# Four resident groups ordered by one account of all engines, and a Strassen-form LSTM step, in a four-layer fp32 graph network kernel

## The chip, the cores and the metric

The kernel runs on one core of one Trainium2 chip. The metric is the device time of one execution in microseconds (us), given as the median of several runs. All arithmetic is fp32. The engines are TensorE (PE in the profile, with its weight loads as PEld), VectorE (DVE), ScalarE (ACT), GpSimd (POOL) and SyncE (SP), which issues the transfers.

## What is computed

The input is 128 graphs of 64 nodes with 256 features, 8192 rows in all, and one 64 x 64 adjacency matrix. Four layers follow each other, each of the form "x = layernorm(x + layer(x))". Cut to what matters, with `mix` for the product over the 64 nodes:

```python
# layer 0: three convolutions with adj*adj, 256 -> 512 -> 1024 -> 256
h = relu(mix(adj*adj, x @ W1)); h = relu(mix(adj*adj, h @ W2)); y = mix(adj*adj, h @ W3)
# layer 1: U holds the eigenvectors of a normalised Laplacian of adj
y = mix(U, relu(mix(U.T, x) @ W1 + b1) @ W2 + b2)
# layer 2: two convolutions, then for p = 1..4 an LSTM over windows of p node rows
h = relu(mix(adj, x @ Wg0 + bg0)); h = relu(mix(adj, h @ Wg1 + bg1))
for p in 1, 2, 3, 4:                       # the last state replaces the last row of each window
    for t in range(p):
        i, f, g, o = split(x_t @ Wih[p].T + hs @ Whh[p].T + bias)
        c = sigmoid(f) * c + sigmoid(i) * tanh(g); hs = sigmoid(o) * tanh(c)
# layer 3: attention over the 64 nodes, masked by adj
h = x @ W + b_lin; y = softmax(where(adj, h @ h.T * adj, -1e16)) @ h + b
```

## The kernel before

The 8192 rows are 64 tiles of 128 rows (two graphs each), and four tiles make a group, so there are 16 groups. All 64 tiles stay in SBUF, in `X`.

**Stage one** (to about 860 us in the profile) does layer 0 for all groups in turn, two groups overlapping, while DVE works through the eigenvectors (`eigen`). Layer 0's big product already has Strassen's form: seven products of quarter matrices in place of eight.

**Stage two** does layers 1, 2 and 3 for each group. The functions are generators, `layer1` (L962), `layer2` (L1057), `lstm` (L992) and `layer3` (L1102), and `group` (L1188) runs them for one group. A loop at the end of the kernel keeps `WAYS = 3` generators going. It counts PE's time in `now[0]`: `mm` (L715 to L718) adds two passes of each matmul, and every `yield` says from when the generator can go on. The stated delays are constants (`MOVE, MIXED, LIN, CONV, NORM, SOFT` and `CELL`), so PE's order is written out by an account of PE alone, in which the other engines are fixed delays. DVE, ACT and POOL are not in it (`manual_schedule(engines={PE})`): their order comes from the tile framework. The last two groups are in `ENDING`; their layer 3 is split into two halves so that the end has more pieces to interleave.

Line L716 is the helper through which nearly all matmuls go. An fp32 matmul leaves two records in the profile, a transpose (L926) one. In the LSTM, L1030 is the tanh of a gate out of PSUM on ACT, L1034 to L1041 are the cell's products on DVE, and L1051 writes the last state into `hT`. One step with t > 0 makes, for each of two halves h of the hidden units and each of four gates, two matmuls with `wih` and two with `whh` into one PSUM tile. For p = 2, 32 windows of 8 rows give n = 256 moving columns, so the second step of that pass is 32 matmuls of 256 columns for each group. A norm is bn_stats and bn_aggr on DVE (L551, L552), two steps on POOL (L553, L554) and the scaling on DVE (L564).

PSUM has eight tiles of one bank each (512 fp32 values for each partition), `ps`. In this kernel every `ps` tile is first written completely by PE and then read.

Of the kernel before, what the change touches and what calls it, by code (L numbers as in the profile page):

```python
# [1 line left out]

# [13 lines left out]
N = 64  # L16
# [24 lines left out]
class Timed:  # L41
# [6 lines left out]
    def __getattr__(self, name):  # L48
        def give(out, *args, **kw):
            self.free[0] = max(self.free[0], self.until[0]) + self.least + 0.0009 * max(0, np.prod(out.shape[1:]) - 64)  # L50
            return getattr(self.engine, name)(out, *args, **kw)  # L51

        return give

# [479 lines left out]
P = 128  # L534
D = 256
EPS = 1e-5
WAYS = 3
ENDING = (14, 15)
LEAD = 10
# [57 lines left out]
def kernel(  # L597
# [51 lines left out]
    X = keep.tile([P, NT, D], F32, name="X")  # L649
# [4 lines left out]
    nc.scalar.dma_start(X[:, 2:4, :], x_t[:, 2:4, :])  # L654
    for t in range(2):
        nc.sync.dma_start(X[:, t, :], x_t[:, t, :])
# [6 lines left out]
    for t in range(4, NT, 2):  # L663
        nc.sync.dma_start(X[:, t:t + 2, :], x_t[:, t:t + 2, :])
# [79 lines left out]
    def layer0(g):  # L744
        xs = X[:, 4 * g:4 * g + 4, :]
# [108 lines left out]
        for t in (2, 0):  # L854
            p = tl(psa, [P, 2, D], "ps", bufs=6)
            mm(p, sqT2, s3[:, t:t + 2, :])
            yield now[0]
            x2 = xs[:, t:t + 2, :]
            VL.tensor_add(x2, p, x2)
            norms.extend(scalar_norm(tc, small, x2, half, spare))  # L860

# [45 lines left out]
    pg = ctx.enter_context(tc.tile_pool(name="pg", bufs=WAYS, reuse_waits="tile"))  # L907
    pw = ctx.enter_context(tc.tile_pool(name="pw", bufs=5, reuse_waits="tile"))
    pv = ctx.enter_context(tc.tile_pool(name="pv", bufs=4, reuse_waits="tile"))
    psb = ctx.enter_context(tc.tile_pool(name="psb", bufs=8, space=bass.MemoryType.PSUM, reuse_waits="tile"))  # L910
# [10 lines left out]
    now[0] = due[0] = 0.0  # L921
    MOVE, MIXED, LIN, CONV, NORM, SOFT = 1.2, 1.2, 1.5, 1.8, 5.2, 5.2
    CELL = {256: 3.8, 168: 2.2, 128: 1.9}

    def turn(out, in_):
        PE.transpose(out, in_, ident)  # L926
        now[0] += 0.11

    def work():
        return tl(pw, [P, 1024], "w")  # L930

    def work2():
        return tl(pv, [P, 512], "v")

    spare[0] = lambda: work2()[:, :D]

    def ps4(shape=(P, 512)):
        return tl(psb, list(shape), "ps")
# [4 lines left out]
    def mixed(src, rhs, ready):  # L943

        dst = as3(work(), 2)
        ps = [ps4() for _ in range(2)]
        for t in range(4):
            if t % 2 == 0:
                yield ready[t // 2]
            for c in range(2):  # L950
                mm(ps[c][:, t * P:(t + 1) * P], src[:, t, c * P:(c + 1) * P], rhs)
        with tc.high_priority(offset=1500):
            V.tensor_copy(dst[:, 0, :], ps[0])
        S.copy(dst[:, 1, :], ps[1])
        yield now[0] + MIXED
        return dst

    def norm(xs, t, ready, more=0.0, scalar=False):
        rows_norm(tc, small, xs[:, t:t + 2, :], half, scalar)
        ready.append(now[0] + NORM + more + (0.8 if ready else 0.0))  # L960

    def layer1(xs, ready):  # L962
        a = yield from mixed(xs, u2, ready)
        for t in range(0, 4, 2):
            V.tensor_add(xs[:, t:t + 2, :], xs[:, t:t + 2, :], ub2.unsqueeze(1).to_broadcast([P, 2, D]))
        h = as3(work2(), 4)
        for t in range(0, 4, 2):
# [5 lines left out]
            yield now[0]  # L973
        yield now[0] + LIN
        z = work2()
        p = ps4((P, 4, P))
        for t in range(4):
            mm(p[:, t, :], h[:, t, :], ut2)
        S.copy(as3(z, 4), p)
        yield now[0] + MOVE  # L980
        ready = []
        for t in range(0, 4, 2):
            p = ps4((P, 2, D))
            for j in range(2):
                mm(p[:, j, :], z[:, (t + j) * P:(t + j + 1) * P], bw2)
            V.tensor_add(xs[:, t:t + 2, :], p, xs[:, t:t + 2, :])  # L986
            norm(xs, t, ready, 2.0)
            yield now[0]
        return ready

    def lstm(hT, p, first, nw):
# [6 lines left out]
        for t in range(p):  # L998
# [4 lines left out]
            G = tl(pg, [P, 2048], "gates")[:, :2 * len(names) * n].rearrange("p (q h n) -> p q h n", h=2, n=n)  # L1003
            gate = {q: G[:, i] for i, q in enumerate(names)}
            units = [(h, q) for h in range(2) for q in names]

            ahead = {}
            early = units[:2] if t else []
            for h, q in early:
                m = slice(("ifgo".index(q) * 2 + h) * P, ("ifgo".index(q) * 2 + h + 1) * P)  # L1010
                ahead[h, q] = pp = ps4()[:, :n]
                for k in range(2):
                    mm(pp, wi[:, k, m], xt[k], k == 0, False)
            if t:
                yield ready
            if p > 1 and not t:
                c = tl(pg, [P, 512], "c")[:, :2 * n].rearrange("p (h n) -> p h n", h=2)
            new = None if last else tl(pg, [P, 512], "hs")[:, :2 * n].rearrange("p (h n) -> p h n", h=2)
            for h, q in units:
                j = 2 * "ifgo".index(q) + h  # L1020
                m = slice(j * P, (j + 1) * P)
                pp = ahead.get((h, q))
                if pp is None:
                    pp = ps4()[:, :n]
                    for k in range(2):
                        mm(pp, wi[:, k, m], xt[k], k == 0, k == 1 and not t)
                if t:
                    for k in range(2):
                        mm(pp, wh[:, k, m], hs[:, k, :], False, k == 1)
                S.activation(gate[q][:, h, :], pp, AF.Tanh, bias=bias[:, j:j + 1], scale=0.5 if q == "g" else 0.25)  # L1030
                if q == "g":
                    to = gate["g"][:, h, :] if t or p == 1 else c[:, h, :]
                    if t:
                        V.scalar_tensor_tensor(c[:, h, :], gate["f"][:, h, :], 1.0, c[:, h, :], op0=ALU.add,  # L1034
                                               op1=ALU.mult)
                    V.scalar_tensor_tensor(to, gate["i"][:, h, :], 1.0, gate["g"][:, h, :], op0=ALU.add, op1=ALU.mult)  # L1036
                    if t:
                        V.scalar_tensor_tensor(c[:, h, :], c[:, h, :], 0.5, to, op0=ALU.mult, op1=ALU.add)  # L1038
                    S.activation(gate["i"][:, h, :], c[:, h, :] if p > 1 else to, AF.Tanh, scale=0.5)  # L1039
                if q == "o" and not last:  # L1040
                    V.scalar_tensor_tensor(new[:, h, :], gate["o"][:, h, :], 1.0, gate["i"][:, h, :], op0=ALU.add,  # L1041
                                           op1=ALU.mult)
                if q == "o":
                    if h == 0:
                        yield now[0]
                elif h == 1 or len(units) == 8:
                    yield now[0]
            if last:

                for h in range(2):  # L1050
                    V.scalar_tensor_tensor(hT[:, h, slice(first + p - 1, first + nw * p, p), :],  # L1051
                                           gate["o"][:, h, :].rearrange("p (w b) -> p w b", b=8), 1.0,
                                           gate["i"][:, h, :].rearrange("p (w b) -> p w b", b=8), op0=ALU.add,
                                           op1=ALU.mult)
            ready = now[0] + CELL[n]
            hs = new
        return ready  # L1057

    def layer2(xs, g, ready):
        a = yield from mixed(xs, adT2, ready)  # L1060
        g1 = as3(work(), 4)
        ready = []
        for t in range(0, 4, 2):
            p = ps4((P, 2, D))
            for j in range(2):
                run(p[:, j, :], [(a[:, k, (t + j) * P:(t + j + 1) * P], cw0[:, k, :]) for k in range(2)])
            V.tensor_add(g1[:, t:t + 2, :], p, wide["c_b0"].unsqueeze(1).to_broadcast([P, 2, D]))
            relu(g1[:, t:t + 2, :], g1[:, t:t + 2, :])
            ready.append(now[0] + CONV)
            yield now[0]  # L1070
        a = yield from mixed(g1, adT2, ready)
        hT = tl(pw, [P, 1024], "w").rearrange("p (k n b) -> p k n b", k=2, b=8)
        for c in range(2):
            p = ps4((P, 4, P))
            run(p, [(cw1[:, k, c * P:(c + 1) * P], a[:, k, :]) for k in range(2)])
            h = work2()
            V.scalar_tensor_tensor(as3(h, 4), rs_row.unsqueeze(1).to_broadcast([P, 4, P]), cb1[:, c:c + 1], p,
                                   op0=ALU.mult, op1=ALU.add)
            S.activation(hT[:, c, :, :].rearrange("p n b -> p b n"), as3(h, 8), AF.Relu, scale=2.0)
            yield now[0]  # L1080
        ready = now[0] + CONV
        for p, first, nw in ((1, 0, 32), (1, 32, 32), (2, 0, 32), (3, 0, 21), (4, 0, 16)):
            if first == 0:
                yield ready
            ready = yield from lstm(hT, p, first, nw)
        hb = as3(work(), 2)
# [175 lines left out]
```

## Time and profile before

| what | value |
|---|---|
| median of 3 runs | 2536.85 us (2536.6 to 2537.04) |
| the profiled execution | 2540.87 us |
| its span, first to last instruction | 2539.1 us |
| granted TensorE clock, mean | 0.993 |
| DVE, ACT in the stretch 910 to 1195 us | 119.05 and 136.85 us busy of 285 |
| POOL's norm steps L553 and L554 | 284 and 705 ns each |
| group outputs to DRAM | 28 transfers of 256 KB, 8 of 128 KB, 2.1 and 1.7 us to landing |

The profile is one execution; its span stands for the chip's work and the 1.8 us around it are start and end. Busy PE time covers each record from start to a modelled end, and records overlap: a record of 128 columns is 275 ns long, but the next one starts about 112 ns after it. What a matmul costs is therefore read from the distance between starts, and short gaps on PE are hidden in the overlap.

### The profile page before, as it was taken

How to read it: one execution, taken by the hardware profiler on the slowest of the kernel's cores; microseconds unless marked ns; L12 is line 12 of the kernel's file. 1: busy time of each engine (PE TensorE's matmuls, PEld its weight loads, DVE VectorE, ACT ScalarE, POOL GpSimd, SP SyncE). 2: the span in 40 equal slices, each digit the busy share in tenths (PEclk: the TensorE clock that was granted, in tenths of full speed). 3: DMA queues.
4: the chain of work that ended last, by engine and by line, in shares of the span. 5: the costliest groups of instructions: out<-in, count | busy, mean ns of one | idle time of the engine just before them, and what ended most of it. 6: DMA issues, size and time to landing. Idle time of an engine off the chain costs nothing.

```text
span 2539.1 us, 39015 instructions
## 1 busy us (share of the span) xinstructions
PE 2494.8 (98%) x15020; PEld 2196.2 (86%) x15020; DVE 1407.8 (55%) x4996; ACT 1090.6 (43%) x2706; POOL 134.2 (5%) x316
## 2 busy tenths in 40 slices
PE   9999999999999999999999999999999999999997
PEld 7788887888878889998989889898998998978996
DVE  6888777778885433454453543544445345353235
ACT  2344333433333344445344444444444534535454
POOL 0000000000000100000000000000000000010001
PEclk9999999999999999999999999999999999999998
DMA  6000000000000300000000000000000000000000
GB/s 219 1 1 1 1 1 1 1 1 1 1 1 1 117 1 1 10 9 1 9 9 1 9 1 10 9 1 9 1 9 9 1 9 9 1 9 1 1 1 26
DMA packets 24634, 32.09 MB, mean 13 GB/s; under 512 B 2176, under 2 KB 21376, under 8 KB 24448
## 3 DMA queue, kind: packets, MB, share of 16 engines
q1 hardware_dynamic: 24096, 29.32, 3.4%
q8 instruction: 118, 1.93, 0.3%
q14 instruction: 68, 0.56, 0.1%
q10 hardware_dynamic: 352, 0.28, 0.0%
HBM read 21.20 MB, written 8.39 MB: 12 GB/s over the span
## 4 chain that ended last, share of the span: by engine, by line
PE 91%; DVE 5%; POOL 2%; issue 1%; DMA 0%; ACT 0%; SPq 0%; ACTq 0%; POOLq 0%; DVEq 0%
PE ps L716 88%; PE ps L926 2%; POOL ln_rs L554 1%; DVE X L564 1%; DVE ln_st L551 1%; DVE D L51 1%; PE ps L1146 1%; PE pc L93 1%; DMA X<-in_x_dram 0%; POOL ln_rs L553 0%; DVE tw L51 0%; DVE ln_mv L552 0%; DVE X L1176 0%; DVE X L986 0%; DVE X L1096 0%
## 5 line engine op out<-in xcount | busy, mean ns | idle before, releaser
L716 PE MATMUL ps<-w,wih 128*128 128x256 f32 (+2 forms) x4992 | 894.0, 319 | 1.8 <-DVE w L1051 1.8
L716 PEld LDWEIGHTS ps<-w,wih 128*128 128x128 f32 x4992 | 760.9, 191 | 47.8 <-issue 5.7
L1030 ACT ACTIVATE gates<-ps,cbi 128x128 f32<-128x128 f32 (+2 forms) x1248 | 499.3, 410 | 523.3 <-PE ps L716 516.2
L716 PE MATMUL ps<-hs,whh 128*128 128x128 f32 (+2 forms) x3072 | 540.5, 303 | 6.2 <-DVE hs L1041 6.2
L716 PEld LDWEIGHTS ps<-hs,whh 128*128 128x128 f32 x3072 | 453.9, 191 | 32.9 <-issue 11.2
L1036 DVE SCALAR_TENSOR_TENSOR gates<-gates 128x256 f32<-128x256 f32 (+2 forms) x256 | 89.3, 349 | 297.4 <-ACT gates L1030 297.4
L716 PE MATMUL ps<-aw,h 128*128 128x256 f32 x1024 | 227.2, 379 | 0.0
L716 PEld LDWEIGHTS ps<-aw,h 128*128 128x128 f32 x1024 | 192.9, 190 | 25.9 <-ACT h L725 0.5
L725 ACT ACTIVATE h<-h 128x512 f32<-128x512 f32 x128 | 80.5, 629 | 170.0 <-DVE h L51 169.8
L1039 ACT ACTIVATE gates<-c 128x128 f32<-128x128 f32 (+2 forms) x288 | 98.1, 341 | 114.1 <-DVE c L1038 87.9
L1034 DVE SCALAR_TENSOR_TENSOR c<-gates,c 128x128 f32<-128x128 f32 (+2 forms) x192 | 62.6, 326 | 139.4 <-ACT gates L1030 138.2
L1051 DVE SCALAR_TENSOR_TENSOR w<-gates 128x256 f32<-128x256 f32 (+2 forms) x160 | 59.6, 376 | 108.5 <-PE ps L716 73.5
L716 PE MATMUL ps<-ss,tw 128*128 128x256 f32 x512 | 117.9, 380 | 0.0
L716 PE MATMUL ps<-ss,aw 128*128 128x256 f32 x512 | 117.3, 379 | 0.0
L716 PE MATMUL ps<-m,aw 128*128 128x256 f32 x512 | 117.1, 380 | 0.0
L716 PE MATMUL ps<-aw,m 128*128 128x512 f32 x256 | 114.8, 594 | 0.0
L1041 DVE SCALAR_TENSOR_TENSOR hs<-gates 128x128 f32<-128x128 f32 (+2 forms) x192 | 62.6, 326 | 93.6 <-ACT gates L1039 52.4
L553 POOL TENSOR_SCALAR ln_rs<-ln_mv 128x2 f32<-128x2 f32 x96 | 26.2, 273 | 1558.4 <-DVE ln_mv L552 1557.9
L716 PEld LDWEIGHTS ps<-ss,aw 128*128 128x128 f32 x512 | 96.6, 190 | 12.8
L716 PEld LDWEIGHTS ps<-ss,tw 128*128 128x128 f32 x512 | 96.3, 190 | 12.9 <-issue 0.2
L564 DVE TENSOR_SCALAR X<-X,ln_mv,ln_rs 128x256 f32<-128x256 f32 x176 | 64.7, 410 | 75.9 <-POOL ln_rs L554 75.9
L716 PEld LDWEIGHTS ps<-m,aw 128*128 128x128 f32 x512 | 95.6, 190 | 12.6 <-issue 0.5
(294 smaller groups left out, 3107.4 us busy)
## 6 DMA issues: line engine op xcount, KB each, us to landing
X<-in_x_dram SPq DMA_DIRECT2D x30, 256.0 KB, 6.3
out_dram<-X SPq DMA_DIRECT2D x28, 256.0 KB, 2.1
wih<-in_c_ih_dram SPq DMA_DIRECT2D x4, 1024.0 KB, 7.2
aw<-in_a_w_dram SPq DMA_DIRECT2D x3, 1024.0 KB, 10.3
whh<-in_c_hh_dram SPq DMA_DIRECT2D x3, 1024.0 KB, 9.4
out_dram<-X SPq DMA_DIRECT2D x8, 128.0 KB, 1.7
aw<-in_a_w_dram SPq DMA_DIRECT2D x1, 512.0 KB, 5.8
cw<-in_c_w_dram SPq DMA_DIRECT2D x2, 256.0 KB, 5.1
```

The source lines that it names most:

```text
L51: return getattr(self.engine, name)(out, *args, **kw)
L553: nc.gpsimd.tensor_scalar(rs, mv[:, :, 1], EPS, None, op0=ALU.add)
L564: nc.vector.tensor_scalar(x[:, t, :], x[:, t, :], mv[:, t, 0:1], rs[:, t:t + 1], op0=ALU.subtract, op1=ALU.mult)
L716: PE.matmul(out, lhsT, rhs, start=start, stop=stop)
L725: S.activation(dst, src, AF.Relu)
L926: PE.transpose(out, in_, ident)
L1030: S.activation(gate[q][:, h, :], pp, AF.Tanh, bias=bias[:, j:j + 1], scale=0.5 if q == "g" else 0.25)
L1034: V.scalar_tensor_tensor(c[:, h, :], gate["f"][:, h, :], 1.0, c[:, h, :], op0=ALU.add, op1=ALU.mult)
L1036: V.scalar_tensor_tensor(to, gate["i"][:, h, :], 1.0, gate["g"][:, h, :], op0=ALU.add, op1=ALU.mult)
L1039: S.activation(gate["i"][:, h, :], c[:, h, :] if p > 1 else to, AF.Tanh, scale=0.5)
L1041: V.scalar_tensor_tensor(new[:, h, :], gate["o"][:, h, :], 1.0, gate["i"][:, h, :], op0=ALU.add, op1=ALU.mult)
L1051: V.scalar_tensor_tensor(hT[:, h, slice(first + p - 1, first + nw * p, p), :], gate["o"][:, h, :].rearrange("p (w b) -> p w b", b=8), 1.0, ...
```

## The change

It has four parts.

1. **One account.** The generators become plain functions which only note operations. `Noted` stands in for an engine and passes each call to `Plan.note` with a duration; `Plan.run` then takes, again and again, the operation that can start earliest on any engine by the account's own clocks, emits it, and advances that engine. PE, DVE, ACT and POOL all follow the account's order (`manual_schedule` now names all four). Which operation must wait for which is found from the elements of a tile that each one touches (`mask`), and tiles get their buffers (`slots`) in the account too. A run of one product's matmuls (`run`) is one entry.
2. **Four groups on the way**, `WAYS = 4`, with gate tiles of half the size. `X` holds 32 tiles. Stage one works on groups 8 to 15 first, writes each finished one to a DRAM buffer (`rest`) and loads groups 0 to 7 in its place (`change`); stage two takes groups 0 to 7 first and loads a waiting group back when one is finished (`Q.dma_start(xs, rest[g])`).
3. **The second step of p = 2 in Strassen's form** (`second`): windows are cut into two halves of 128 columns and the gates into two pairs; `add_weights` makes four sums of weight blocks once (eight DVE additions of 512 columns), and for each group eight DVE subtractions of 128 columns make the moving operands. For each half h seven products follow, each of two gates, 128 columns and two addends (`wih`, `whh`). `two` puts two products into one PSUM tile, products (1, 2), (6, 7), (5, 3) and then 4 alone; one ACT copy and seven DVE additions of 256 columns put them together, and the tanh reads the sums from SBUF.
4. **Small things.** Layer 1's second mixing is noted by pairs of tiles, the copy before layer 2's transposes is cut in two by batches, each output tile is a transfer of its own, and layer 3's transposes for `hn` come after the scores. What is left of stage one's norms (`left_over`) is handed to the account as a group 0.

```diff
+class Plan:
+    LAG = {"PE": 0.205, "DVE": 0.16, "ACT": 0.15, "POOL": 0.0, "SP": 2.0}
+    MOST = {"w": 3, "v": 2, "ps": 4, "gates": 2}
+    OWN = {"PE": 0.0, "DVE": 0.125, "ACT": 0.105, "POOL": 0.0, "SP": 0.0}
...
+    def note(self, engine, calls, cost, ready=0.0):
...
+                t, write = x.tile, i == 0
+                mask = np.zeros(int(np.prod(t.shape[1:])), bool)
+                mask[x.at.reshape(-1)] = True
+                for other, w, rows, m in t.past:
+                    if (w or write) and other is not op and other.start is None and rows[0] < x.rows[1] and x.rows[0] < rows[1] and (m & mask).any():
+                        op.before.add(other)
...
+    def run(self, groups, ways):
...
+                if first:
+                    t0 = min(t for t, _ in first)
+                    t, op = min((x for x in first if x[0] <= t0 + 0.02), key=lambda x: (rank(x[1]), x[1].rank))
+                    if best is None or t < best[0]:
+                        best = t, op
...
+            self.emit(op)
...
-WAYS = 3
+WAYS = 4
...
-    X = keep.tile([P, NT, D], F32, name="X")
+    X = keep.tile([P, NT - 4 * LATE, D], F32, name="X")
...
+        def change():
+            nc.sync.dma_start(rest[g], xs)
+            for t in (0, 2):
+                nc.sync.dma_start(xs[:, t:t + 2, :], given(order[g + LATE])[:, t:t + 2, :])
...
+    def second(hT, xt, hs, c, bias):
...
+        moving = ((x1[0], h1[0]), (x2[0], h2[0]), (x2[1], h2[1]), T4, T1, T2, T3)
+        weight = (0, 1, 6, 2, 3, 4, 5)
+        for h in range(2):
...
+            def two(*which):
+                p = ps4((P, 2, 2, P))
+                for at, i in enumerate(which):
+                    for q in range(2):
+                        run(p[:, at, q, :], [(ways[s][weight[i]][:, q, h, :], moving[i][s]) for s in range(2)])
+                return p[:, 0], p[:, 1]
+            p1, p2 = two(0, 1)
+            S.copy(u1, p1)
+            V.tensor_add(a, u1, p2)
+            p6, p7 = two(5, 6)
+            V.tensor_add(c12, u1, p6)
+            V.tensor_add(b, c12, p7)
+            p5, p3 = two(4, 2)
+            V.tensor_add(d, b, p5)
+            V.tensor_add(c12, c12, p5)
+            V.tensor_add(c12, c12, p3)
+            p4, _ = two(3)
+            V.tensor_add(b, b, p4)
...
-    with tc.manual_schedule(engines={mybir.EngineType.PE}):
...
+    with tc.manual_schedule(engines={mybir.EngineType.PE, mybir.EngineType.DVE, mybir.EngineType.Activation,
+                                     mybir.EngineType.Pool}):
+        plan.run([left_over] + [lambda g=g: group(g) for g in range(NT // 4)], WAYS)
```

## The prediction

> **What bounds the kernel now.** I read the page's first part and the chain of waits first.
>
> ```profile
> span 2539.1 us, 39015 instructions
> ...
> PE 2494.8 (98%) x15020; PEld 2196.2 (86%) x15020; DVE 1407.8 (55%) x4996; ACT 1090.6 (43%) x2706; POOL 134.2 (5%) x316
> ...
> PE 91%; DVE 5%; POOL 2%; issue 1%; DMA 0%; ACT 0%; SPq 0%; ACTq 0%; POOLq 0%; DVEq 0%
> ```
>
> PE is the bound: 98% busy, 91% of the chain that ended last. Work taken from PE shortens the time, and every new PE wait lengthens it. Next, by windows, where PE is not busy in stage two (columns: window, length, then busy time of PE, PEld, DVE, ACT, POOL, granted clock, DMA share, GB/s):
>
> ```profile
> 860.00:910.00 50.00, 45.87 (x273) 40.41 (x272) 29.28 (x73) 22.53 (x51) 7.70 (x18) 0.93 0.26 105
> ...
> 1200.00:1436.00 236.00, 235.72 (x1561) 213.26 (x1561) 110.14 (x310) 106.80 (x263) 13.63 (x28) 1.00 0.02 8
> 1436.00:1442.00 6.00, 3.92 (x30) 3.43 (x28) 4.53 (x17) 1.27 (x4) 2.43 (x4) 1.00 0.02 5
> ...
> 2255.00:2271.00 16.00, 10.25 (x57) 9.69 (x56) 8.34 (x24) 3.46 (x8) 3.12 (x6) 0.68 0.06 20
> 2271.00:2500.00 229.00, 228.16 (x1567) 213.28 (x1565) 86.58 (x257) 112.20 (x287) 8.30 (x20) 1.00 0.01 2
> 2500.00:2532.00 32.00, 23.09 (x147) 17.51 (x145) 18.66 (x66) 14.86 (x38) 5.38 (x16) 0.79 0.08 25
> ```
>
> PE stands still only at four kinds of place: the stage change, five group boundaries (1436 to 1442 is one; the others are like it, 2.1 to 2.4 us idle each), the boundary before the last groups, and the end. DVE is under half busy between them.
>
> What a matmul costs is read from starts in PE's timeline (start, busy, records):
>
> ```profile
> 1511.95 2.75 PE L716 MATMUL ps<-w,wih 128*128 128x256 f32 x12
> 1514.54 0.27 PE L926 MATMUL ps<-ident,w 128*128 128x128 f32 x1
> ...
> 2471.76 1.06 PE L716 MATMUL ps<-hs,whh 128*128 128x128 f32 x8
> 2472.66 0.59 PE L716 MATMUL ps<-w,dw 128*128 128x512 f32 x1
> ```
>
> Twelve records of 256 columns take 2.59 us, 0.216 each; eight of 128 take 0.90, 0.112 each. By this pitch all PE records together, form by form, are 2477 us. So of the span 3 us lie before the first matmul, 8 after the last one, and 51 are lost between: 7 in stage one, 8 at the stage change (4.1 idle, the rest from a clock of 0.93), about 14 at the boundaries (11.4 idle by windows, and some 0.24 that overlap hides at each of ten waits), 9 at 2255 to 2271 (5.75 idle, the rest from a clock of 0.68), 15 in the last 32.
>
> **Strassen's matmuls.** Out go 32 matmuls of 256 columns for each group, 512 in all, of two records each: 1024 x 0.216 = 221.2 us. In come 2 halves x 7 products x 2 gates x 2 addends = 56 of 128 columns, 896 in all: 1792 x 0.112 = 200.7 us. PE saves 20.5 us, wholly on the path. That is less than an eighth (27.6), as 128 columns cost more than half of 256.
>
> **Its DVE and ACT work.** For each group DVE gets 8 subtractions of 128 columns (0.29 by the row of the hidden state's product), 14 additions of 256 (0.41 by the row below) and slightly dearer final products (0.3), about 8.4 us in some 100; ACT gets two copies, 0.7. DVE goes from 45% to about 54%: no new bound. The eight sums of weights (0.68 each for 512 columns, 5.5 us) are held back 30 us in the account; both weights were issued by 859 in the trace, so they cost nothing unless DVE's queue meets them before they landed. Without that cover the stage change pays up to 5.5.
>
> **The new waits.** This decides the sum. The account tracks PSUM by element; the built program does not. A `two` tile is one bank. I laid out the built order and counted places where PE writes into a PSUM tile that another engine has already begun to read: before has none in 2142 tiles, the changed kernel has 69. A typical case: PE writes product 6, then the first gate of 7; DVE's addition of 6 stands there; PE's second gate of 7 waits for it. That addition in turn waits for PE's last matmul before it. In 41 of the 69 no other PE work stands between that matmul and the waiting one, in 5 one pair of matmuls (0.45), in 23 at least 0.9. Per group this is one wait in the first half h and two in the second. Queued behind the waiting matmul is all of PE.
>
> The Trainium skill has the rule that speaks against this change: "PSUM — Partial Sum Buffer", section "PSUM bank collisions raise a hardware error", wants accesses guarded by bank and quadrant, not by address. By it these waits must exist; by the account, which looks at addresses, they are free and the change gains 32 us more. The trace of before shows no such wait, so it cannot settle it; the waits stand in the built program, and I count them.
>
> The nearest rows are the ping-pong at the end (PE, a copy of 256 columns, PE) and the addition that layer 1 makes out of PSUM:
>
> ```profile
> 2528.27 0.63 PE L926 MATMUL ps<-ident,att 128*128 128x128 f32 x2
> ...
> 2528.99 0.37 ACT L1166 COPY v<-ps 128x256 f32<-128x256 f32 x1 [2.64 <-PE ps L926]
> ...
> 2529.42 0.80 PE L716 MATMUL ps<-w,v 128*128 128x256 f32 x1 [0.52 <-ACT v L1166]
> ```
> ```profile
> L971 DVE TENSOR_TENSOR v<-ps,wide_b_b 128x256 f32<-128x256 f32 x22 | 9.1, 414 | 3.5 <-PE ps L716 3.5
> ```
>
> PE's record outlasts its pitch by 0.275 - 0.112 = 0.16; reader start after it 0.09; the addition 0.41; PE's restart 0.06; and after a wait the first two records of 128 start 0.07 further apart (0.18 after the boundary wait at 1438). Sum 0.8 at the half clock of those rows; I take 0.75. Bounds: 0.58 (tail and addition alone) and 1.1 (half of a 0.69 us operation ahead on DVE). 41 x 0.75 + 5 x 0.3 = 32 us, between 24 and 46.
>
> Do these waits also lower the clock? "TensorE: Matmul & The Clock Gate", section "What's actually happening", says an idle window of about 3.4 us halves it. The rows: 2.08 idle in 6 us left the clock at 1.00; 2.8 and 3.0 close together brought 0.68. Three waits of 0.75 within 7 us are like the former, so I add nothing. Were each group throttled for one such window, it would be 16 x 1.7 = 27 us more.
>
> **What the order takes away.** The boundary waits follow norm and hidden-state chains of 4 to 5 us for which three groups lacked filler. The new order keeps four groups and prices DVE and ACT near the trace (0.334 + 0.16 for an addition with hand-over, the trace 0.414 and some 0.07). I let the boundaries go from 14 to 4, not to nothing, because chains now stand hardly further apart than they last; what is late next is the hidden state. The spot at 2255 goes from 9 to 2. At the stage change four first layers interleave, but the first group's chain (matmuls 14, copies, norm and hand-overs 12 by their rows) has only 30 us of PE before its first LSTM matmul: 8 to 5. At the end all of groups 13, 14 and 15 reach layer 3 in the last 28 us of PE work; DVE has by its rows about 41 us from there on for 34 of PE's, and 8 us after PE's last matmul where before has 2.5. So 23 (15 and the 8 of drain) goes to 21 only. Together -22; bounds: -32 (all recoverable gaps but drain) and 0 (gaps reappear in the tight order, each engine in fixed order).
>
> **At nothing.** Eight stores of 512 KB and eight later loads sit on SP's queue behind norms whose rows are next read some 400 us later; stage-two reloads wait on outputs, and the next outputs behind them come 90 us later. If that cover failed, one transfer would show its 6.3 us. SP's weight loads stand behind changes done 300 us earlier. Stage one: unchanged.
>
> **Sum.** -20.5 + 32 - 22 = -10.5 on the profiled 2540.87, so 2530.4. The median lies 4.0 lower than that execution; from 2536.85 it gives 2526.
>
> **Rivals.** (a) The bank waits are hidden (PE would have idled there, or readers come early): -42.5, less some 8 that tight chains keep, 2502. For: 23 of 69 already have cover. Against: the other 41 have none in the order. (b) The order does not do what it says: boundary and end gaps stay in new places; -20.5 + 32 - 6: 2542. For: margins are thin; against: the account's durations fit the rows. (c) Slower: the mid-bank reader queues on DVE, now in a fixed order behind another group's operation that itself waits. Each of the 41 waits then costs more than 0.75 + 10.5/41 = 1.0 us for equality, over 1.13 for a measurable loss; at 1.3 it is 2536.85 - 10.5 + 23 = 2549. For: DVE is over half busy around `second`; against: its own chain is there alone by the account.
>
> **Chances.** Main case 0.57 (2516 to 2536), (a) 0.17, (b) 0.14, (c) 0.12. About 0.2%, 5 us, is what a measurement of this kernel can tell from no change. Faster by more: most of the main case and (a), 0.68; within: its upper edge and part of (b), 0.20; slower: (c) and a little of (b), 0.12. The range takes half of (a) in and most of (b): 2504 to 2545.
>
> **What would show it.** PE records: 512 fewer of 256 columns with `whh`, about 2457 us by pitch. In the list of waits, PE for the DVE additions of `second`: about 46 times, visible idle 0.5 to 0.6 each (the overlap hides the rest), some 25 us. No row of 2 us idle at boundaries. DVE about 54%. If PE shows no such waits, the main step is wrong and (a) holds; if they are above 0.8 idle each, (c). If the last 60 us show over 25 idle, the end is mis-sized.

## The result and the profile after

The changed kernel takes 2521.59 us (median of 4 runs, 2521.0 to 2522.03) against 2536.72 us for the kernel before, run beside it on the same chip (2535.9 to 2537.04). The ratio is 0.9941, with a 95% interval of 0.9923 to 0.9958. That is 15.1 us less; the prediction said 10.5 less. The profiled execution took 2522.03 us and its span is 2520.3 us, 18.8 us less than the span before.

The page's first part and the head of its chain, for the changed kernel:

```profile
span 2520.3 us, 41153 instructions
...
PE 2473.2 (98%) x15788; PEld 2194.3 (87%) x15788; DVE 1523.3 (60%) x5404; ACT 1105.1 (44%) x2754; POOL 139.4 (6%) x317
...
PE 91%; DVE 6%; DMA 1%; ACT 1%; issue 1%; POOL 0%; SPq 0%; ACTq 0%; POOLq 0%; DVEq 0%
```

PE is still the bound, with the same shares as before. So this page alone does not tell that anything was gained or lost inside; the windows do (columns as before: busy time of PE, PEld, DVE, ACT, POOL, granted clock, DMA share, GB/s):

```profile
860.00:910.00 50.00, 50.00 (x318) 44.79 (x317) 35.48 (x83) 29.99 (x72) 7.61 (x17) 1.00 0.27 105
...
1200.00:1436.00 236.00, 229.95 (x1671) 212.69 (x1671) 129.56 (x383) 106.74 (x266) 15.84 (x30) 1.00 0.04 14
1436.00:1442.00 6.00, 6.00 (x38) 5.69 (x36) 3.64 (x9) 4.64 (x12) 0.00 (x0) 1.00 0.00 0
...
2255.00:2271.00 16.00, 16.00 (x82) 11.59 (x81) 7.31 (x12) 6.53 (x9) 0.00 (x0) 1.00 0.00 1
```

These windows are the same stretches of time as before, in which the groups now stand elsewhere, so they show that PE is busy at full clock there, but not by themselves that every boundary is shut. And the body between boundaries, where PE was busy 235.72 of 236 us, now shows 6 us of idle time. The list of PE's waits over the whole span settles both (line, what was waited for; us in total, times, longest). Its head before, the waits at the stage change, the boundaries and the spot at 2255:

```profile
PE ps L716 <- DVE X L564: 6.9, 5, 2.8
PE ps L716 <- DVE hs L1041: 6.2, 5, 1.3
PE ps L716 <- ACT v L725: 4.4, 3, 3.0
```

and after:

```profile
PE ps L154 <- DVE gates L154: 22.7, 41, 0.7
...
PE ps L154 <- DVE hs L154: 1.7, 2, 0.9
...
PE ps L154 <- ACT v L154: 1.0, 2, 0.5
```

The first row is the additions of `second`: 41 waits with 22.7 us of visible idle time, 0.55 each. By the timeline 27 of them are of 0.51, 12 of 0.70 and 2 of 0.18. Such a row did not stand in the list before. The last row is two waits of the same kind for another reader: PE is about to write more of product 2 into the tile out of which ACT still copies product 1. (In the built order 50 of the 69 counted places have an addition as the reader and 19 this copy.)

To compare kernels I sum, as in the prediction, each PE record's usual distance to the next start (the median of its form), and call the rest "lost". Us of the profiled executions; e1, e3, e4, e5 and e6 are told of below:

| part of the span | before | after | e1 | e3 | e4 | e5 | e6 |
|---|---|---|---|---|---|---|---|
| PE records at their pitch | 2476.6 | 2456.0 | 2476.5 | 2456.1 | 2456.1 | 2476.6 | 2456.1 |
| lost in stage one | 6.9 | 7.2 | 7.1 | 7.2 | 7.0 | 7.3 | 7.1 |
| lost at the stage change, 850 to 900 | 8.1 | 0.2 | 0.2 | 0.2 | 0.2 | 1.2 | 1.2 |
| lost from 900 to 2200 | 11.6 | 33.6 | -1.1 | -2.5 | 10.1 | 6.5 | 22.5 |
| lost from 2200 to 2400 | 9.0 | 3.4 | -0.2 | 0.0 | 2.2 | -0.3 | -0.1 |
| lost from 2400 on | 15.9 | 2.9 | 5.7 | 3.0 | 3.0 | 5.6 | 4.0 |
| before the first and after the last matmul | 11.1 | 17.0 | 16.9 | 16.9 | 17.0 | 17.0 | 16.9 |
| span | 2539.1 | 2520.3 | 2505.1 | 2480.8 | 2495.6 | 2513.9 | 2507.7 |

The small negative entries mean that a median is a touch longer than most of its records; 1 to 3 us in 1300 is the error of this sum.

### The profile page after: what moved, and what is told of

It is laid out like the page before. It is cut to its first block, busy times and chain, and to the rows that moved or that the text cites. A ratio compares the mean times of both kernels' runs of the same rounds, so it can differ in the third digit from the quotient of the medians.

```text
span 2520.3 us, 41153 instructions
## 1 busy us (share of the span) xinstructions
PE 2473.2 (98%) x15788; PEld 2194.3 (87%) x15788; DVE 1523.3 (60%) x5404; ACT 1105.1 (44%) x2754; POOL 139.4 (6%) x317
## 4 chain that ended last, share of the span: by engine, by line
PE 91%; DVE 6%; DMA 1%; ACT 1%; issue 1%; POOL 0%; SPq 0%; ACTq 0%; POOLq 0%; DVEq 0%
PE ps L154 60%; PE ps L926 30%; DVE gates L154 2%; ACT gates L154 1%; DVE D L52 1%; DVE X L154 1%; PE pc L286 1%; DMA aw<-in_a_w_dram 0%; DVE c L154 0%; DVE tw L52 0%; POOL rs L154 0%; DVE st L154 0%; DVE w L154 0%; DMA bw<-in_b_w_dram 0%; DMA X<-in_x_dram 0%
## 5 line engine op out<-in xcount | busy, mean ns | idle before, releaser
L154 PE MATMUL ps<-w,wih 128*128 128x128 f32 (+2 forms) x4864 | 839.1, 309 | 1.0 <-ACT v L154 1.0
L154 PEld LDWEIGHTS ps<-w,wih 128*128 128x128 f32 x4864 | 726.6, 191 | 34.7 <-issue 5.0
L154 ACT ACTIVATE gates<-ps,cbi 128x128 f32<-128x128 f32 (+2 forms) x1120 | 447.6, 403 | 508.1 <-PE ps L154 498.2
L154 PE MATMUL ps<-hs,whh 128*128 128x128 f32 (+1 forms) x2816 | 459.3, 286 | 1.7 <-DVE hs L154 1.7
L154 PEld LDWEIGHTS ps<-hs,whh 128*128 128x128 f32 x2816 | 394.9, 191 | 5.4 <-DVE hs L154 3.4
L154 PE MATMUL ps<-w,sums 128*128 128x128 f32 x896 | 122.5, 280 | 22.7 <-DVE gates L154 22.7
L154 PEld LDWEIGHTS ps<-w,sums 128*128 128x128 f32 x896 | 108.8, 192 | 31.5 <-DVE gates L154 30.7
L154 ACT ACTIVATE gates<-gates,cbi 128x256 f32<-128x256 f32 x128 | 54.9, 497 | 157.8 <-DVE gates L154 157.6
L154 POOL TENSOR_SCALAR rs<-mv 128x2 f32<-128x2 f32 x96 | 25.6, 267 | 1530.3 <-DVE mv L154 1529.1
L926 PEld LDWEIGHTS ps<-ss,tw 128*128 128x128 f32 x512 | 96.3, 190 | 12.9 <-issue 0.2
```

The source lines that it names most:

```text
L154: getattr(e, name)(*[real(x) for x in args], **{k: real(v) for k, v in kw.items()})
L926: PE.matmul(out, lhsT, rhs, start=start, stop=stop)
```

## The experiments

**Theory.** The order closes the gaps and Strassen's matmuls save some 20 us, but PE pays for each write into a PSUM tile that DVE is already reading. **Rivals.** DVE's additions come late for reasons of their own (its queue, or the eight PSUM tiles are too few), so separate tiles would not help; or Strassen's form is worth its 20 us as built, and leaving it out costs that.

**e1: Strassen's form left out.** The second step of p = 2 is computed in the plain form; order and four groups stay.

```diff
-PAIRS = True
+PAIRS = False
```

> The account of all engines and four groups alone; the second step of p = 2 is made as before, with 32 matmuls of 256 columns a group. Theory (the readers in the middle of a PSUM bank cost about 33 us, the Strassen matmuls save 20.5): 2521.6 + 20.5 - 33 = 2509 us, no PE wait for a DVE addition. Rival (the waits replace idle time that PE would have had anyway in this order, so they are worth little): 2521.6 + 20.5 = 2542 us, with other PE waits where those stood.

Measured: 2505.42 us, ratio to before 0.9875 (0.986 to 0.989). Leaving the form out makes the kernel 16.2 us *faster*, and the rival's 2542 is refuted. Its 20.5 us of saved matmuls come back in the table (2476.5 against 2456.0), but the 33.6 us lost from 900 to 2200 are gone. The order alone is thus worth 31.6 us, and Strassen's form as built costs 16.

**e2: the account sees a PSUM tile as one piece.** Operations on a `ps` tile count as touching all of it, so that the account itself orders the reader behind the tile's last write. The built kernel has the same operations and tiles, in another order.

```diff
                 mask[x.at.reshape(-1)] = True
+                if t.tag == "ps":
+                    mask[:] = True
```

> The changed kernel, but the account treats every touch of a PSUM tile as a touch of the whole tile, so that a reader is placed after all writes of its bank; same instructions, other order. Theory: the 69 writes after a reader fall to none, and 2521.6 - 33 = 2489 us. Rival (DVE is late for its own reasons): PE's waits for DVE move elsewhere and the time stays above 2515 us.

Measured: 2484.96 us, ratio 0.9794 (0.9779 to 0.9808). PE's list of waits holds no row for the additions any more. That is 36.6 us less, 4 more than was said.

**e3: each product in a PSUM tile of its own.** Now the tile that PE writes is never one that DVE reads; half of each tile stays unused.

```diff
-                p = ps4((P, 2, 2, P))
-                for at, i in enumerate(which):
+                ps = [ps4((P, 2, P)) for _ in which]
+                for p, i in zip(ps, which):
                     for q in range(2):
-                        run(p[:, at, q, :], ...)
-                return p[:, 0], p[:, 1]
+                        run(p[:, q, :], ...)
+                return ps
```

> The changed kernel, but each of the seven products gets a PSUM tile of its own, seven for each half in place of four. Theory: no write after a reader, 2521.6 - 33 = 2489 us, within 4 us of the account by bank. Rival (the fuller PSUM makes PE wait for buffers instead): above 2505 us.

Measured: 2482.66 us (2482.29 to 2482.75), ratio 0.9784 (0.9767 to 0.98): the best of all kernels, 54.4 us under before and 38.9 under the changed kernel. The eight tiles of PSUM suffice. The same place in both, first in the changed kernel (timeline: start, busy, engine, line, records of a group; idle before it and what ended it in brackets; other engines' and weight-load rows left out):

```profile
1314.72 1.50 PE L154 MATMUL ps<-w,sums 128*128 128x128 f32 x12
...
1316.26 0.42 DVE L154 TENSOR_TENSOR gates<-v,ps 128x256 f32<-128x256 f32 x1 [0.85 <-PE ps L154]
1316.73 0.94 PE L154 MATMUL ps<-w,sums 128*128 128x128 f32 x6 [0.51 <-DVE gates L154]
1317.48 0.42 DVE L154 TENSOR_TENSOR gates<-gates,ps 128x256 f32<-128x256 f32 x1 [0.80 <-PE ps L154]
```

and in e3:

```profile
1303.70 2.17 PE L154 MATMUL ps<-w,sums 128*128 128x128 f32 x18
1304.79 0.42 DVE L154 TENSOR_TENSOR gates<-v,ps 128x256 f32<-128x256 f32 x1 [0.40 <-PE ps L154]
1305.69 2.21 DVE L154 TENSOR_TENSOR gates<-gates,ps 128x256 f32<-128x256 f32 x5 [0.47 <-PE ps L154]
1305.71 0.39 PE L154 MATMUL ps<-hs,sums 128*128 128x128 f32 x2
```

In the first, DVE waits for PE until 1316.26, PE then waits for DVE until 1316.73, and DVE for PE again: two engines that take turns. In e3, PE runs 18 records and goes on while the same additions, of the same 0.42, run beside it. The rival that DVE is late for reasons of its own is refuted: DVE has the same work there and PE does not notice. A small share of it is true, though. The second of the three waits of a group, 1323.06 in the changed kernel, is one of the twelve of 0.70:

```profile
1322.38 0.29 DVE L154 SCALAR_TENSOR_TENSOR w<-gates 128x128 f32<-128x128 f32 x1 [0.21 <-ACT gates L154]
1322.59 0.41 DVE L154 TENSOR_TENSOR gates<-v,ps 128x256 f32<-128x256 f32 x1
...
1323.06 1.83 PE L154 MATMUL ps<-w,sums 128*128 128x128 f32 x14 [0.70 <-DVE gates L154]
```

Here the addition starts without a pause behind another operation of DVE, the write of the first half's state. That makes these waits 0.19 longer than the others, 2.3 us in all.

One reservation holds for e2 and e3: with other rules for the tiles the account lays out the whole order anew, so they change more than the waits. e4 does not.

**e4: only products 6 and 7 in tiles of their own.** The dose.

```diff
-            p6, p7 = two(5, 6)
+            (p6, _), (p7, _) = two(5), two(6)
```

> A dose: only products 6 and 7 get separate PSUM tiles, (1, 2) and (5, 3) still share one. By the order, 28 of the 41 uncovered waits go and 13 stay. Theory: 28 x 0.8 = 22 us less, 2499 us, with PE's wait for DVE down from 22.7 to about 7 us. Rival (the first wait only shields a later one of the same half): 2510 us or more.

Measured: 2496.9 us (2496.46 to 2497.41), ratio 0.984 (0.9825 to 0.9855). PE's order stays that of the changed kernel: 99.9% of its records have the same tiles at the same place. Of 41 waits 15 are left, 13 of 0.51 (as many as were said to stay) and the 2 of 0.18:

```profile
PE ps L154 <- DVE gates L154: 7.0, 15, 0.5
```

26 waits fewer, in the same order, gave 24.7 us, 0.95 each; the other 15, from here to e3, are worth 14.2 us, 0.95 each. So the loss goes with the waits. That both steps give 0.95 is in part chance: at the matmuls of the `sums` weights themselves PE's starts show 22.9 us (0.88 each) for the first step and 11.4 (0.76) for the second. (Counted in the built order as in the prediction, the writes into a tile with a reader fall from 69 to 38 here, and there are none in e1, e2 and e3.)

**e5 and e6: three groups on the way.** How much of the order is the account, and how much the fourth group? Without Strassen's form (e5), and with it in tiles of its own (e6):

```diff
-WAYS = 4
+WAYS = 3
```

> The second step of p = 2 in the plain form and three groups on the way in place of four; of the change only the account, the eight waiting groups and the small things stay. Theory: what closed the gaps is that DVE, ACT and POOL are in the account with durations near their rows, and the fourth group adds a little filler: 2509 us (2507 to 2515), some 4 us over the run without Strassen's form and four groups (2505.4). Rival: the fourth group is the filler that the boundaries lacked; then about 15 us of boundary gaps and 8 us at the spot at 2255 come back and the time is 2520 to 2530, with rows of 2 us of idle PE at group boundaries.

> Each of Strassen's products in a PSUM tile of its own, and three groups on the way in place of four. Theory: with the waits gone the fourth group matters little here too: 2487 us (2483 to 2494), some 4 us over the same kernel with four groups (2482.7). Rival: Strassen's step has a longer chain outside PE (about 8 us of DVE for each group), and three groups leave no filler for it: 2498 to 2510, with the loss in the groups' middle, at the LSTM's second pass.

Measured: e5 2514.1 us (2512.82 to 2515.64), ratio 0.9912 (0.9899 to 0.9926), e6 2509.61 us (2509.49 to 2511.27), ratio 0.9896 (0.9882 to 0.9909). The theory holds for e5, at the upper edge of its range: against before, the account and the other parts bring 22.4 us without the fourth group, and the fourth group brings 8.7 more (2514.1 to 2505.42), where 4 was said. For e6 the theory falls and the rival holds: here the fourth group is worth 27.0 us (2509.61 to 2482.66), and with three groups Strassen's form saves only 4.5. PE's own work is that of e3; the loss is PE waiting (lines of e6 from 1100 to 2200: group, then busy and mean ns, idle before it):

```profile
L154 PE MATMUL ps<-w,wih 128*128 128x168 f32 x968 | 166.1, 307 | 12.2 <-DVE w L154 12.2
...
L154 PE MATMUL ps<-w,cw 128*128 128x512 f32 x86 | 41.7, 606 | 4.0 <-DVE w L154 4.0
```

The first row is the matmuls with 168 columns, which are the LSTM's pass of p = 3. One such wait, in e6's timeline, with what it waits for:

```profile
1318.47 1.89 PE L154 MATMUL ps<-bw,v 128*128 128x256 f32 x8
...
1322.13 0.48 DVE L154 SCALAR_TENSOR_TENSOR w<-gates 128x128 f32<-128x128 f32 x2
...
1322.67 5.11 PE L154 MATMUL ps<-w,wih 128*128 128x168 f32 x34 [1.13 <-DVE w L154]
```

Strassen's last product ends at about 1318.5. After it follow the last addition, activations, cell products and the write of the new state at 1322.13 to 1322.61, some 4.1 us (in which DVE also does pieces of other groups' layers) in which PE needs work of other groups. Three groups do not have enough of it there; four do.

**e7 and e8: the end.** Both have tiles of their own for the products. In e7 three groups instead of two have layer 3 in halves; the same setting also moves work of group 13 from DVE to ACT, above all the scaling of its last two norms, with more POOL steps. In e8 DVE does the scaling of the last norms but for the first piece, in place of ACT.

```diff
-ENDING = (14, 15)
+ENDING = (13, 14, 15)
```

```diff
-            norm(x2, g in ENDING)
+            norm(x2, g in ENDING and t == 0 and first == 0)
```

> Each of Strassen's products in a PSUM tile of its own, and the last three groups in place of two have layer 3 in halves. Against the same kernel with two such groups (2482.7): if the end is held by the last groups' chains coming in large pieces, smaller pieces of group 13 let PE finish up to 3 us sooner and the time is 2479 to 2481. If the end is held by the work that DVE, ACT and POOL have left after PE's last matmul (14 us), the pieces change nothing or add fixed costs: 2482 to 2485.

> Each of Strassen's products in a PSUM tile of its own, and in the last two groups the scaling of the last norms on DVE but for the first piece, where ACT did it. If the 14 us after PE's last matmul are a chain of steps that hand over between engines, one hand-over less gives 1 to 2 us: 2481. If they are DVE's own work (it is busy 6.9 of 7 us there), the added scalings lengthen it: 2484 to 2487.

Measured: e7 2494.96 us (2493.31 to 2495.79), ratio 0.9836 (0.9822 to 0.9849), e8 2483.68 us (2483.38 to 2484.56), ratio 0.9793 (0.9779 to 0.9806). e7 is 12.3 us slower than e3, outside both expectations: it loses 4.7 us from 2200 to 2400 and 17.4 after, with single waits of 2.9 to 3.2 us on DVE and ACT and a granted clock of 0.57 from 2300 to 2304 and 0.52 from 2447 to 2454, and saves 6 after the last matmul. That PE waits there is shown; why the account lays out the smaller pieces so, and which of the two things that the setting changes does it, was not followed further. e8 lies 1.0 us above e3, but their ratios to before lie within each other's intervals, so no change is shown. In its profile the tail is 0.8 us shorter (13.7 to 12.9 from the end of the last matmul), and PE loses 1.9 us more ahead of it. Most of the tail stays open.

Not tried: all of `X` kept in SBUF under the new order, which would price the parking of groups in DRAM by itself; SBUF did not have the room. The trace shows no PE wait on these transfers.

## Why the prediction was right

The forecast of 2526 lay 4.4 us above the result, and its mechanism, waits against saved matmuls and closed gaps, is the one the runs show. Point by point:

- **Strassen's matmuls, -20.5.** Right: the records' pitches sum to 2456.0 after 2476.6. Measured as a whole, without waits, the form saves 22.8 (2505.42 to 2482.66; 2.7 of it at the end, where e1 is looser), so its DVE and ACT work costs nothing under four groups.
- **DVE and ACT work, no new bound.** Right. DVE rose from 44% to 51% of stage two (702.66 us busy in 910 to 2500 before, 790.76 in 910 to 2460 after) where 54% was said. The sums of weights cost nothing: the stage change, where they lie, loses 0.2. What the prediction did not see is the price of the form's longer chain when the filler is short; e6 shows it, at 18 us more than e5 gives for the same step from four groups to three (27.0 against 8.7). It did not matter here, since four groups stayed.
- **The new waits, +32.** The mechanism was right, and the count nearly: 46 waits were forecast, 41 full and 5 half covered; the trace has 39 of full length and 2 short ones for DVE, and 2 for ACT. That the account holds these writes free, which e2 mends in two lines, is nearly the whole loss (36.6 of 38.9). Too small was the price of one. From e3 to the changed kernel it is 38.9 us, or 0.95 for each of the 41, where 41 x 0.75 + 5 x 0.3 was said, with bounds of 24 to 46. Directly at the waits PE's starts show 34.3 us, 0.84 each: the prediction's own rows summed to 0.8, and taking 0.75 instead was not borne out. Some 3.8 more is lost at four other waits that e3 does not have: the two for ACT's copy, and two of 0.86 for a hidden state (at 1213.37 and 2139.18), which were not in the sum. Visible idle time, 0.55 each, was as said.
- **Hidden waits, rival (a).** Refuted by the 41 rows and by e2 and e3. **A longer queue on DVE, rival (c).** Refuted as a size, not as a mechanism: at 12 of the 41 waits the addition does queue behind another operation on DVE, but PE's idle time there is 0.70, under the 0.8 that was named as the sign of (c), and by PE's starts these waits cost 0.97 each, just under the 1.0 at which the change would have gained nothing by that sum. At the other 29 the idle time is 0.51 or less.
- **The clock, nothing added.** Right: it stays at 1.00 in every window of the changed kernel above, with waits of 0.51, 0.70 and 0.51 at 1316.73, 1323.06 and 1325.62.
- **What the order takes away, -22.** Too small, and rival (b), which would have had the gaps back, is refuted. From before to e3 the stage change goes from 8.1 to 0.2 (said: 5 left), the boundaries from 11.6 to none (said: 4 left), the spot at 2255 from 9.0 to 0.0 (said: 2 left), and the end with its tail from 24.0 to 16.9, when 3 us ahead of the first matmul are taken off (said: 21 left). That is 38 us of spans, 4 of which belong to the execution profiled before, which was slower than its median; e1, whose end is 2.7 us looser, gives 31.6 for the order by medians, close to the bound of 32. The step that failed is "chains now stand hardly further apart than they last": it holds for three groups (e5 still loses 6.5 from 900 to 2200), not for four (e1 loses nothing there). With three groups the order gave 22.4 (e5), just what was forecast for four. At the stage change, pieces of layer 1 and layer 2 of several groups alternate and the first LSTM matmul starts at 890.81, where before it started at 903.6; I had let the first group's chain bound it.
- **The end, 8 us of drain.** PE now finishes its work with hardly a gap (2.9 lost after 2400) and what is left after it grew from 8 to 14. The prediction had DVE's 8 us of work there; DVE ends 6.8 us after the last matmul (2513.41), but POOL and ACT go on with the norms until 2517.44 and the last outputs land after that, which it had not added.

So two sizes were off in opposite directions: the order gave more by about 12 (38 less 4, against 22) and the waits took 7 more. Their difference is what separates 2526 from 2521.6. That the forecast came so close is thus in part luck.

## What to carry to other kernels

When a scheduler decides an engine's order, what it tracks must be no finer than what the built program tracks: here it tracked elements of PSUM where the program tracks tiles, and 41 places that it held free cost 0.84 us each at the spot; with what followed from them 38.9 us went, 1.5% of the kernel. Such places can be counted before any run, by going through the built order for writes into a tile that has already a reader. A form that saves matmuls but lengthens the chain behind the last of them is only worth its saving when enough other work is on the way (here 4.5 us with three groups and 22.8 with four); change the two together, or measure the one under both.

## What was not expected of the hardware

A wait's visible idle time was 0.55 us, but the time lost at the spot was 0.84, so the idle column understates such a wait by about a third. And the clock does not go by the idle time in total. The changed kernel idles for 22.7 us in 41 pieces of at most 0.71 and keeps 1.00. The kernel before was granted 0.5 after a wait of 2.77 us which ended at 2259.78. Here are its windows around that wait:

```profile
2255.00:2257.00 2.00, 2.00 (x18) 1.80 (x16) 1.45 (x5) 0.47 (x1) 0.85 (x2) 1.00 0.07 23
2257.00:2259.00 2.00, 0.01 (x1) 0.00 (x0) 1.42 (x6) 0.00 (x0) 0.72 (x2) 1.00 0.39 131
2259.00:2261.00 2.00, 1.22 (x5) 1.22 (x6) 1.69 (x6) 0.00 (x0) 0.28 (x1) 0.50 0.00 0
```

PE stands still from about 2257, and from 2259 on the clock is at 0.50, before the wait is over: it fell after some 2.0 us of standing still. "TensorE: Matmul & The Clock Gate", section "What's actually happening", of the Trainium skill puts the idle window at about 3.4 us; this one is shorter, so here the measured wait decides. Nor does it take one long wait. At the stage change of the kernel before, no wait was longer than 1.45 us:

```profile
880.00:900.00 20.00, 17.34 (x83) 14.29 (x82) 10.69 (x31) 5.15 (x11) 4.76 (x11) 0.83 0.00 1
...
888.46 1.16 PE L716 MATMUL ps<-adT,w 128*128 128x128 f32 x8 [1.22 <-ACT w L725]
...
891.07 2.08 PE L716 MATMUL ps<-adT,w 128*128 128x128 f32 x8 [1.45 <-ACT w L725]
```

Within these 20 us the clock was granted at 1.00 until 890 and at 0.50 from 892 to 896. Waits of 1.03 and 1.34 us at 1438.63 and 1442.28 left it at 1.00. These traces do not show how short or how far apart waits must be to be safe.
